# One queue for W1, another order of the first products, and another order of the last small operations in a conditional adapter kernel

## The chip, the cores and the metric

The kernel runs on one core of a Trainium2 chip. The metric is the time of one execution on the device in microseconds (us); before the change it is 321.33 us, the median of three runs (320.34 to 324.42). One further execution was recorded by the hardware profiler, and all views come from it.

## The reference

128 samples x[b] of 128 rows by 512 columns (float32), each with a language number between 0 and 9. The language picks its own weights: W1 (512 by 128), W2 (128 by 512), and the vectors b1, b2, gamma, beta. For each sample:

```
h       = relu(x @ W1[lang] + b1[lang])            # 128 x 128, the product "down"
adapted = h @ W2[lang] + b2[lang]                  # 128 x 512, the product "up"
y       = x + adapted
normed  = (y - mean(y)) / sqrt(var(y) + 1e-5)      # over the 512 columns
out     = x + normed * gamma[lang] + beta[lang]
```

## The kernel before

**What is resident.** All ten languages' W1 and W2 stay in SBUF (`w1`, `w2`, 2.62 MB each), and so do beta, gamma and b2, each spread over all 128 partitions (`beta_b`, `gamma_b`, `b2_b`). The spreading is done at the start by `spread(r, copier)` (L152): for each of the 30 rows TensorE multiplies a selection column with the rows' parts into a PSUM buffer of the pool `p_y` (five buffers), and VectorE or ScalarE copies that to SBUF (L161, L159). x comes in groups of four samples (1 MB each) into four buffers; the first group comes in two halves (`load_part`, L82).

**The start's transfers.** Two engines issue transfers, each on a queue of its own: SyncE (q1 in the profile) and ScalarE (q10). W1 goes in four parts of 655,360 bytes, one for each slice of 128 rows of all ten languages; its contiguous runs are 512 bytes long. The loop at L95 puts parts 0 and 1 on SyncE and parts 2 and 3 on ScalarE. SyncE's queue goes on with x's second half, W2 in two transfers, and x_1, x_2, x_3 (L100 to L109). x and W2 have runs of 2 KB.

**One sample's work.** `stage_w1` (L184): ScalarE copies the sample's W1 from `w1` at a place given by a register, so it needs all four parts. `transpose_x` (L189): four transposes on TensorE into the single buffer of pool `p_x`. `copy_xT` (L194): ScalarE brings them to SBUF. `down` (L211): four products into the single buffer of pool `p_h`. `relu` (L221) on ScalarE. `up` (L225): the product with W2, into a `p_y` buffer, with a small product for b2 first where `b2_by_matmul` says so (samples 0 to 3, then every fourth). `residual` (L235), `negative_mean`, `scale` and `finish` are VectorE's, `square` and `deviation` ScalarE's; GpSimd adds x and b2 beforehand (`add_b2`, L198), and x and beta (`add_beta`, L204). The reciprocal standard deviation comes out of the five small VectorE steps `rstd_1` to `rstd_5`, for two samples at once; for the last four samples `rstd_of(b, n)` (L307) does step n for one sample alone.

**What sets the order.** The tile framework places the waits. Nearly every instruction is passed through `keep` (L43), which holds it behind the one written before it on the same engine; so each engine's order is the written one.

**The start's order (L425 to L453).** Idle products (`spin`) for TensorE, the transposes of sample 0, rows 0 to 21 of the spreading with the transposes of sample 1 between them, `stage_w1` of samples 0 and 1, four more idle products, then a loop over samples 0 to 2: `down`, the transposes two samples on, `relu`, `copy_xT`, up to three rows of the spreading (copied by VectorE), `stage_w1` two samples on. After it `up(0)`, `up(1)`, `down(3)`, `relu(3)`, `stage_w1(5)`. The main loop (L455) begins with `up(2)` and the transposes of sample 4.

**The end (`tail`, L355).** The last five samples leave the loop's pattern. At its last step, the sample called b + 1 is the last (127) and b the one before; their small steps stand between the scalings (`scale`) and the two last `finish_last` (L350), each of which is followed by a store.

Of the kernel before, what the change touches and what calls it, by code (L numbers as in the profile page):

```python
# [16 lines left out]
P = 128  # L17
# [6 lines left out]
def cond_resid_kernel(ctx: ExitStack, tc: tile.TileContext, x, itok, W1, b1, W2, b2, gamma, beta, out):  # L24
# [8 lines left out]
    nc = tc.nc  # L33
    B, S, H = x.shape
# [8 lines left out]
    def keep(ins):  # L43

        engine = ins.ins.engine
        if engine in last:
            tc.add_manual_dep(ins.ins, last[engine], behind, reason="kept order")
        last[engine] = ins.ins.name
        return ins
# [27 lines left out]
    w1 = const.tile([P, L, KC, A], FP, name="w1")  # L77
# [15 lines left out]
    nc.vector.memset(warm, 1.0)  # L93
    keep(nc.scalar.activation(warm, warm, AF.Sqrt))
    for k in range(KC):  # L95
        queue = nc.sync if k < 2 else nc.scalar
        keep(
            queue.dma_start(out=w1[:, :, k, :], in_=W1[:, k * P : (k + 1) * P, :].rearrange("l p a -> p l a"))
        )
    load_part(2, G)  # L100
    for l in range(0, L, 5):
        keep(
            nc.sync.dma_start(
                out=w2[:, l * H : (l + 5) * H].rearrange("p (l h) -> p l h", l=5),
                in_=W2[l : l + 5].rearrange("l a h -> a l h"),
# [46 lines left out]
    def spread(r, copier):  # L152
        t = (beta_b, gamma_b, b2_b)[r // L]
        row = p_y.tile([P, H], FP, tag="y", name=f"row_{r}")
        pick_r = pick[:, r : r + 1].to_broadcast([96, P])
        keep(nc.tensor.matmul(row, lhsT=pick_r, rhs=parts[:96, :], start=True, stop=True))  # L156
        dst = t[:, r % L * H : (r % L + 1) * H]
        if copier is nc.scalar:
            keep(nc.scalar.copy(dst, row))  # L159
        else:  # L160
            keep(nc.vector.tensor_copy(dst, row))  # L161
# [4 lines left out]
    def lid(b, engine):  # L166
        g = b // G
        if (g, engine) not in lids:
            loads, vals = nc.values_load_multi_w_load_instructions(  # L169
                lang[0:1, g * G : (g + 1) * G],  # L170
                engines=[engine],
                min_val=0,
                max_val=L - 1,
                skip_runtime_bounds_check_because="clamped on the chip to 0..L-1 above",
            )
            for ins in loads:
                keep(ins)
            lids[g, engine] = vals
        return lids[g, engine][b % G]
# [4 lines left out]
    def stage_w1(b):  # L184
        w1s[b] = wp.tile([P, KC, A], FP, tag="w1s", name=f"w1s_{b}")
        src = w1.rearrange("p l k a -> p (l k a)")[:, bass.ds(lid(b, ET.Activation) * (KC * A), KC * A)]
        keep(nc.scalar.copy(w1s[b].rearrange("p k a -> p (k a)"), src))  # L187
# [23 lines left out]
    def down(b):  # L211
        phs[b] = p_h.tile([P, P], FP, tag="h", name=f"ph_{b}")
        for k in range(KC):
            keep(
                nc.tensor.matmul(  # L215
                    phs[b], lhsT=w1s[b][:, k, :], rhs=xT[b][:, k, :], start=(k == 0), stop=(k == KC - 1)
                )
            )
        del xT[b], w1s[b]

    def relu(b):  # L221
        hT[b] = tp.tile([P, P], FP, tag="hT", name=f"hT_{b}", bufs=6)
        keep(nc.scalar.activation(hT[b], phs.pop(b), AF.Relu, bias=b1T[:, bass.ds(lid(b, ET.Activation), 1)]))  # L223
# [11 lines left out]
    def residual(b):  # L235
        r = xb(b) if b2_by_matmul(b) else rs.pop(b)
        s = st.tile([P, 1], FP, tag="sum", name=f"sum_{b}")
        keep(nc.vector.scalar_tensor_tensor(ys[b], ys[b], 1.0, r, ALU.mult, ALU.add, accum_out=s))  # L238
        sums[b] = s

    def negative_mean(b):
        nmeans[b] = st.tile([P, 1], FP, tag="nmean", name=f"nmean_{b}")
        keep(nc.vector.tensor_scalar(nmeans[b], sums.pop(b), -1.0 / H, None, ALU.mult))  # L243
# [15 lines left out]
    def rstd_1(g):  # L259
        stats[g] = p_s.tile([P, 6], FP, tag="s", name=f"stat_{g}")  # L260
        keep(nc.vector.tensor_scalar(stats[g][:, 0:2], ssqs.pop(g), -0.5 / H, -0.5 * EPS, ALU.mult, ALU.add))

    def rstd_2(g):
        y0s[g] = st.tile([P, 2], FP, tag="y0", name=f"y0_{g}")
        keep(nc.vector.reciprocal(y0s[g], sds.pop(g)))

    def rstd_3(g):
        keep(nc.vector.tensor_tensor(stats[g][:, 2:4], stats[g][:, 0:2], y0s[g], ALU.mult))

    def rstd_4(g):  # L270
        keep(nc.vector.tensor_tensor(stats[g][:, 4:6], stats[g][:, 2:4], y0s[g], ALU.mult))  # L271

    def rstd_5(g):
        rstds[g] = st.tile([P, 2], FP, tag="rstd", name=f"rstd_{g}")
        keep(
            nc.vector.scalar_tensor_tensor(rstds[g], stats.pop(g)[:, 4:6], 1.5, y0s.pop(g), ALU.add, ALU.mult)
        )

    def scale(b):
        v = lid(b, ET.DVE)  # L280
        keep(
            nc.vector.scalar_tensor_tensor(  # L282
                ys[b], ys[b], nmeans.pop(b), gamma_b[:, bass.ds(v * H, H)], ALU.add, ALU.mult
            )
        )
# [20 lines left out]
    def rstd_of(b, n):  # L306

        if not ends:
            ends["t"] = p_s.tile([P, 32], FP, tag="s", name="stat_ends")
        t = ends["t"][:, 8 * (b % 4) : 8 * (b % 4) + 3]  # L310
        if n == 1:
            keep(nc.vector.tensor_scalar(t[:, 0:1], ssqs.pop(b), -0.5 / H, -0.5 * EPS, ALU.mult, ALU.add))
        elif n == 2:
            y0s[b] = st.tile([P, 1], FP, tag="y0", name=f"y0_{b}")
            keep(nc.vector.reciprocal(y0s[b], sds.pop(b)))
        elif n < 5:
            keep(nc.vector.tensor_tensor(t[:, n - 2 : n - 1], t[:, n - 3 : n - 2], y0s[b], ALU.mult))
        else:
            rstds[b] = st.tile([P, 1], FP, tag="rstd", name=f"rstd_{b}")
            keep(nc.vector.scalar_tensor_tensor(rstds[b], t[:, 2:3], 1.5, y0s.pop(b), ALU.add, ALU.mult))  # L320
# [26 lines left out]
    def store_last(b):  # L347
        nc.sync.dma_start(out=out[b], in_=os[b // 2][:, b % 2, :])
# [6 lines left out]
    def tail(b):  # L355
        p = E // 2
        if b == E + 3:
            rstd_of(b - 2, 4)
        residual(b)
        if b == E + 1:  # L360
            rstd_1(p)
            rstd_2(p)
            negative_mean(b)
            rstd_3(p)
            scale(E - 1)
            rstd_4(p)
            rstd_5(p)
            shift(E)
            finish(E - 2)
            store(p - 1)  # L370
            deviation_of(b)
            by_pool(E, False)
        elif b == E + 2:
            negative_mean(b)
            rstd_of(b - 1, 1)
            rstd_of(b - 1, 2)
            finish_last(E - 1)
            store_last(E)
            rstd_of(b - 1, 3)
            deviation_of(b)  # L380
        elif b == E + 3:
            rstd_of(b - 2, 5)
            negative_mean(b)
            shift(b - 2)
            residual(b + 1)
            negative_mean(b + 1)
            by_pool(b - 2, False)
            store_last(b - 2)
            rstd_of(b - 1, 1)
            rstd_of(b - 1, 2)  # L390
            rstd_of(b - 1, 3)
            scale(b - 1)
            deviation_of(b)
            rstd_of(b - 1, 4)
            rstd_of(b - 1, 5)
            scale(b)
            deviation_of(b + 1)
            by_pool(b - 1, True)
            store_last(b - 1)
            rstd_of(b, 1)  # L400
            rstd_of(b, 2)
            rstd_of(b, 3)
            scale(b + 1)
            rstd_of(b, 4)
            rstd_of(b + 1, 1)
            rstd_of(b + 1, 2)
            rstd_of(b, 5)
            rstd_of(b + 1, 3)
            rstd_of(b + 1, 4)
            finish_last(b)  # L410
            rstd_of(b + 1, 5)
            finish_last(b + 1)


    def spin(n, width):
        idle = p_s.tile([P, H], FP, tag="s", name="idle")
        for _ in range(n):
            keep(
                nc.tensor.matmul(
                    idle[:, :width], lhsT=ones, rhs=ones[:, 0:1].to_broadcast([P, width]), start=True, stop=True  # L420
                )
            )
# [12 lines left out]
            spin(1, H // 2)  # L435
    stage_w1(0)
    stage_w1(1)
    spin(4, H)
    for b in range(3):
        down(b)  # L440
        if b < 2:
            transpose_x(b + 2)
        relu(b)
        if b < 2:
            copy_xT(b + 2)
        for r in range(22 + 3 * b, min(25 + 3 * b, R)):
            spread(r, nc.vector)
        stage_w1(b + 2)
    up(0)
    up(1)  # L450
    down(3)
    relu(3)
    stage_w1(5)  # L453

    for i in range(3, B + U):  # L455
        if i < B and i % G == 0 and i // G + 3 < NG:
            load_x(i // G + 3)
        b = i - U - 1
# [20 lines left out]
        p = g - 1  # L479
# [79 lines left out]
```

## Time and profile before

| | |
|---|---|
| median of three runs | 321.33 us |
| the profiled execution | 321.27 us |
| its span, first to last instruction | 319.5 us |
| PE (TensorE) busy | 304.8 us, 95% |
| DVE (VectorE) busy | 302.8 us, 95% |
| ACT (ScalarE) busy | 283.3 us, 89% |
| POOL (GpSimd) busy | 280.7 us, 88% |
| mean DMA rate | 228 GB/s |
| mean granted TensorE clock | 0.991 |

PE stands for TensorE's products, PEld for its weight loads, DVE for VectorE, ACT for ScalarE, POOL for GpSimd, SP for SyncE. L187 is line 187 of the kernel. A line of the timeline gives the start, the duration, the engine, the line of code, the operation, what it writes and reads, and in brackets the engine's idle time before it and what ended that. Operations of one engine overlap in part, so distances are taken from start to start. In the names of tiles buffer numbers are left out: `w<-in_L_cond_W_dram` stands for W1 as well as W2, `b_b` for `b2_b`, `row` for a row of the spreading, `py` for the product up, `ph` for the product down.

### The profile page before, as it was taken

The page shows a single profiled execution, that of the slowest core. Times are in us where ns is not written, and L with a number is a line of the kernel's source. Part 1 is how long each engine was busy: PE and PEld are TensorE (multiplying, and loading weights), DVE is VectorE, ACT ScalarE, POOL GpSimd, SP SyncE. Part 2 cuts the span into 40 slices and gives each one's busy share as a digit, 9 for nine tenths or more (in the row PEclk, how much of TensorE's full clock was granted, in tenths as well). Part 3 has the DMA queues.
Part 4 walks back from the last instruction along what each step waited for, and adds up shares of the span by engine and source line. Part 5 has one row for each costly group of instructions (what it writes and reads, how often), then busy time and mean ns, then how long its engine had stood idle before and what let it go on. Part 6 is the DMA issues. An engine that isn't in the chain of part 4 may idle for free.

```text
span 319.5 us, 7184 instructions
## 1 busy us (share of the span) xinstructions
PE 304.8 (95%) x1890; PEld 226.4 (71%) x1890; DVE 302.8 (95%) x1003; ACT 283.3 (89%) x718; POOL 280.7 (88%) x234
## 2 busy tenths in 40 slices
PE   8979999999999999999999999999999999999960
PEld 3566777777777777777777777777777777777740
DVE  5956999999999999999999999999999999999995
ACT  2556989999999999999999999999999999999972
POOL 1306999999999999999999999999999999999874
PEclk9999999999999999999999999999999999999996
DMA  7997566777566766777666666777666666733234
GB/s 209 321 385 276 199 253 210 265 264 254 205 213 220 241 240 220 257 262 261 224 211 214 233 242 221 248 263 260 223 214 214 223 249 223 244 132 134 111 114 173
DMA packets 40987, 72.89 MB, mean 228 GB/s; under 512 B 1737, under 2 KB 6868, under 8 KB 40946
## 3 DMA queue, kind: packets, MB, share of 16 engines
q1 hardware_dynamic: 38294, 71.07, 64.8%
q10 hardware_dynamic: 2652, 1.36, 1.7%
q8 instruction: 16, 0.26, 0.3%
q14 instruction: 25, 0.20, 0.2%
HBM read 38.86 MB, written 33.55 MB: 227 GB/s over the span
## 4 chain that ended last, share of the span: by engine, by line
POOL 46%; issue 26%; POOLq 9%; DVE 7%; PE 5%; DMA 5%; ACT 1%; ACTq 0%; DVEq 0%
POOL o L209 31%; POOL r L202 14%; POOLq L169 8%; DMA w<-in_L_cond_W_dram 5%; DVE py L282 2%; PE ph L215 2%; DVE py L238 1%; DVE o L291 1%; PE py L232 1%; PE pxT L192 1%; POOLq L209 1%; DVE o L352 1%; PE row L156 1%; ACT w1s L187 0%; PE py L231 0%
## 5 line engine op out<-in xcount | busy, mean ns | idle before, releaser
L209 POOL TENSOR_TENSOR o<-x,beta_b 128x512 f32<-128x512 f32 x128 | 161.8, 1277 | 10.6 <-DVE beta_b L161 10.6
L215 PE MATMUL ph<-xT,w1s 128*128 128x128 f32 x1024 | 135.5, 275 | 1.9 <-ACT w1s L187 1.8
L202 POOL TENSOR_TENSOR r<-x,b_b 128x512 f32<-128x512 f32 x93 | 118.7, 1276 | 21.0 <-DMA x<-in_x_dram 12.1
L232 PE MATMUL py<-w,hT 128*128 x256 | 131.0, 593 | 0.2 <-DVE o L291 0.2
L215 PEld LDWEIGHTS ph<-xT,w1s 128*128 128x128 f32 x1024 | 124.7, 192 | 4.0 <-ACT w1s L187 2.3
L192 PEld LDWEIGHTS pxT<-ident,x 128*128 128x128 f32 x512 | 64.0, 141 | 66.6 <-issue 44.4
L282 DVE SCALAR_TENSOR_TENSOR py<-py,nmean,gamma_b 128x512 f32<-128x512 f32 x126 | 94.7, 751 | 0.0
L291 DVE SCALAR_TENSOR_TENSOR o<-py,rstd,o 128x512 f32<-128x512 f32 x122 | 90.4, 741 | 1.0
L250 ACT ACTIVATE sq<-py,nmean 128x512 f32<-128x512 f32 x124 | 85.2, 687 | 3.0 <-DVE nmean L243 1.8
L196 ACT COPY xT<-pxT 128x512 f32<-128x512 f32 x128 | 73.7, 576 | 11.9 <-PE pxT L192 9.7
L187 ACT COPY w1s<-w 128x512 f32 x128 | 79.4, 621 | 2.1 <-DMA w<-in_L_cond_W_dram 2.0
L192 PE MATMUL pxT<-ident,x 128*128 128x128 f32 x512 | 77.0, 273 | 0.7 <-ACT xT L196 0.7
L238 DVE SCALAR_TENSOR_TENSOR py<-py,r 128x512 f32<-128x512 f32 x93 | 64.7, 696 | 2.4 <-PE pxT L192 0.7
L223 ACT ACTIVATE hT<-ph,b1T 128x128 f32<-128x128 f32 x128 | 47.4, 371 | 4.1 <-PE ph L215 4.1
L232 PEld LDWEIGHTS py<-w,hT 128*128 128x128 f32 x256 | 41.7, 192 | 2.7 <-issue 0.6
L238 DVE SCALAR_TENSOR_TENSOR py<-py,x 128x512 f32<-128x512 f32 x35 | 24.2, 692 | 2.4 <-PE py L232 1.8
L250 ACT ACTIVATION_READ_ACCUMULATOR sq<-py,nmean 128x1 f32 x124 | 25.3, 204 | 0.0
L256 ACT ACTIVATE sd<-ssq,eps 128x2 f32<-128x2 f32 x62 | 18.3, 296 | 2.1
L243 DVE TENSOR_SCALAR nmean<-sum 128x1 f32<-128x1 f32 x128 | 18.8, 147 | 0.2
L231 PE MATMUL py<-parts,pick 96*128 96x512 bf16 x35 | 13.3, 381 | 0.0
L238 DVE DVE_READ_ACCUMULATOR py<-py,r 128x1 f32 x93 | 13.1, 141 | 0.0
L271 DVE TENSOR_TENSOR stat<-stat,y 128x2 f32<-128x2 f32 x62 | 12.8, 206 | 0.0
(54 smaller groups left out, 118.1 us busy)
## 6 DMA issues: line engine op xcount, KB each, us to landing
x<-in_x_dram SPq DMA_DIRECT2D x31, 1024.0 KB, 6.0
out_dram<-o SPq DMA_DIRECT2D x61, 512.0 KB, 3.3
w<-in_L_cond_W_dram SPq DMA_DIRECT2D x2, 1280.0 KB, 15.6
out_dram<-o SPq DMA_DIRECT2D x6, 256.0 KB, 2.0
w<-in_L_cond_W_dram SPq DMA_DIRECT2D x2, 640.0 KB, 6.6
w<-in_L_cond_W_dram ACTq DMA_DIRECT2D x2, 640.0 KB, 8.6
x<-in_x_dram SPq DMA_DIRECT2D x2, 512.0 KB, 3.6
rows<-in_L_cond_beta_dram ACTq DMA_DIRECT2D x1, 20.0 KB
```

Of the source, the lines that this page charges most:

```text
L187: keep(nc.scalar.copy(w1s[b].rearrange("p k a -> p (k a)"), src))
L192: keep(nc.tensor.transpose(pxs[b][:, k, :], xb(b)[:, k * P : (k + 1) * P], ident))
L196: keep(nc.scalar.copy(xT[b], pxs.pop(b)))
L202: keep(nc.gpsimd.tensor_tensor(rs[b], xb(b), b2_b[:, bass.ds(v * H, H)], ALU.add))
L209: keep(nc.gpsimd.tensor_tensor(os[g][:, j, :], xb(b), beta_b[:, bass.ds(v * H, H)], ALU.add))
L215: nc.tensor.matmul(phs[b], lhsT=w1s[b][:, k, :], rhs=xT[b][:, k, :], start=(k == 0), stop=(k == KC - 1))
L223: keep(nc.scalar.activation(hT[b], phs.pop(b), AF.Relu, bias=b1T[:, bass.ds(lid(b, ET.Activation), 1)]))
L232: keep(nc.tensor.matmul(ys[b], lhsT=hT[b], rhs=w2[:, bass.ds(v * H, H)], start=not m, stop=True))
L238: keep(nc.vector.scalar_tensor_tensor(ys[b], ys[b], 1.0, r, ALU.mult, ALU.add, accum_out=s))
L250: keep(nc.scalar.activation(sq, ys[b], AF.Square, bias=nmeans[b], accum_out=ssqs[g][:, j : j + 1]))
L282: nc.vector.scalar_tensor_tensor(ys[b], ys[b], nmeans.pop(b), gamma_b[:, bass.ds(v * H, H)], ALU.add, ALU.mult)
L291: nc.vector.scalar_tensor_tensor(o, ys.pop(b), rstds[g][:, j : j + 1], o, ALU.mult, ALU.add)
```

## The change

Three edits. All four parts of W1 are issued by SyncE, behind x's first half and ahead of its second. In the start's order there is one idle product less (three in place of four); the loop takes in sample 3, so that four products down stand ahead of the first product up; and the copies of rows 23, 26 and 29 go from VectorE to ScalarE. At the end, the small steps of the last two samples are interleaved, and all of them stand ahead of the two last `finish_last`.

```diff
--- before.py
+++ after.py
@@ -93,9 +93,8 @@
     nc.vector.memset(warm, 1.0)
     keep(nc.scalar.activation(warm, warm, AF.Sqrt))
     for k in range(KC):
-        queue = nc.sync if k < 2 else nc.scalar
         keep(
-            queue.dma_start(out=w1[:, :, k, :], in_=W1[:, k * P : (k + 1) * P, :].rearrange("l p a -> p l a"))
+            nc.sync.dma_start(out=w1[:, :, k, :], in_=W1[:, k * P : (k + 1) * P, :].rearrange("l p a -> p l a"))
         )
     load_part(2, G)
     for l in range(0, L, 5):
@@ -399,16 +398,16 @@
             store_last(b - 1)
             rstd_of(b, 1)
             rstd_of(b, 2)
+            rstd_of(b + 1, 1)
+            rstd_of(b + 1, 2)
             rstd_of(b, 3)
+            rstd_of(b + 1, 3)
             scale(b + 1)
             rstd_of(b, 4)
-            rstd_of(b + 1, 1)
-            rstd_of(b + 1, 2)
+            rstd_of(b + 1, 4)
             rstd_of(b, 5)
-            rstd_of(b + 1, 3)
-            rstd_of(b + 1, 4)
+            rstd_of(b + 1, 5)
             finish_last(b)
-            rstd_of(b + 1, 5)
             finish_last(b + 1)
 
 
@@ -435,8 +434,8 @@
             spin(1, H // 2)
     stage_w1(0)
     stage_w1(1)
-    spin(4, H)
-    for b in range(3):
+    spin(3, H)
+    for b in range(4):
         down(b)
         if b < 2:
             transpose_x(b + 2)
@@ -444,13 +443,10 @@
         if b < 2:
             copy_xT(b + 2)
         for r in range(22 + 3 * b, min(25 + 3 * b, R)):
-            spread(r, nc.vector)
+            spread(r, nc.scalar if r % 3 == 2 else nc.vector)
         stage_w1(b + 2)
     up(0)
     up(1)
-    down(3)
-    relu(3)
-    stage_w1(5)
 
     for i in range(3, B + U):
         if i < B and i % G == 0 and i // G + 3 < NG:
```

## The prediction

> **What bounds the kernel now.** I read four views: busy time by stretches, then the waits, then the timeline of ACT and PE around the longest waits, then the end on DVE. First the stretches (start:end, length, then busy time and instructions of PE, PEld, DVE, ACT, POOL, then PE's clock, the DMA share, GB/s):
>
> ```profile
> 5.00:5.50 0.50, 0.50 (x3) 0.22 (x2) 0.47 (x2) 0.00 (x0) 0.00 (x0) 1.00 1.14 346
> 6.00:12.00 6.00, 6.00 (x35) 3.53 (x34) 4.84 (x11) 3.41 (x6) 0.00 (x0) 1.00 1.19 292
> 17.00:29.00 12.00, 10.12 (x62) 7.39 (x62) 7.72 (x17) 7.23 (x16) 2.44 (x2) 1.00 1.05 386
> 36.00:300.00 264.00, 263.94 (x1676) 200.64 (x1675) 260.68 (x880) 251.24 (x647) 255.41 (x207) 1.00 0.67 228
> ```
>
> From 36 to 300 us PE has no gap: starts on the timeline give four transposes 0.44, a product down 0.89, a product up 0.86, a b2 product 0.21, so four batches cost 4 x 2.19 + 0.21 = 8.97 us, which is the period seen. DVE is nearly full, POOL does its seven operations per four batches in about 8.65 us and waits for DVE. So **the loop is bound by PE**, and a PE that enters it earlier ends earlier by as much, if what feeds it keeps up. What counts is the start and the end. The waits (engine and line, what for, us in total, times, longest):
>
> ```profile
> POOL r L202 <- DMA x<-in_x_dram: 12.1, 1, 12.1
> ACT w1s L187 <- DMA w<-in_L_cond_W_dram: 2.0, 1, 2.0
> PE ph L215 <- ACT w1s L187: 1.8, 1, 1.8
> ```
>
> The timeline of ACT, then of PE (start, us, operation, idle before it):
>
> ```profile
> 14.91 0.58 ACT L159 COPY b_b<-row 128x512 f32<-128x512 f32 x1 [0.79 <-PE row L156]
> 17.53 1.14 ACT L187 COPY w1s<-w 128x512 f32 x2 [2.04 <-DMA w<-in_L_cond_W_dram]
> ...
> 15.04 1.36 PE L419 MATMUL idle<-ones 128*128 128x256 bf16 x5
> 18.20 1.16 PE L215 MATMUL ph<-xT,w1s 128*128 128x128 f32 x8 [1.80 <-ACT w1s L187]
> ...
> 27.71 0.60 PE L192 MATMUL pxT<-ident,x 128*128 128x128 f32 x4
> ```
>
> W1 lands at 17.47. ACT is through with its copies at 15.49 and waits; PE is through with its idle products at about 16.0 and waits until 18.20. From 18.20 to 28.15 PE runs without a gap. The transpose of batch 4 (27.71) needs x_1, which landed at 26.5 (POOL's wait above ends at 26.56). Which queue moved what, from 5 to 5.5 us, then from 6 to 12 us (packets, MB, share of the engines):
>
> ```profile
> q1 hardware_dynamic: 338, 0.17, 114.1%
> ...
> q10 hardware_dynamic: 1863, 0.95, 64.7%
> q1 hardware_dynamic: 1586, 0.80, 54.6%
> ```
>
> q1 is SP's queue, q10 ACT's. At 5 to 5.5 us SP's queue was alone, with W1's packets of 512 bytes (0.17 MB / 338), at **346 GB/s**; with both queues full of them the rate was 292. From 12 us on q1 carries 2 KB packets of x and W2, and the last 0.33 MB of W1 on q10 take until 17.
>
> **What the Trainium skill says.** *DMA: Bandwidth & Descriptors*, "Queues, rings and completion order": an engine goes round robin between the queues, packet by packet. The trace agrees (8 to 10 us: 585 and 559 packets); so W1's small packets get a small share beside W2's large ones. Same page, "Issuing engines are not separate DMA queues": a second issuing engine saves only issue time. The trace goes further: the second queue cost 346 - 292 = 54 GB/s. *TensorE: Matmul & The Clock Gate*, "What's actually happening": about 3.4 us of idleness halve PE's clock. The idle 1.80 us left it at 1.00, so one idle product less is harmless. *VectorE: DVE Perf Modes*, "The DRAIN you can't avoid": the next operation waits until the pipeline is empty. The trace differs: independent small operations start 0.06 to 0.07 us apart, dependent ones about 0.19; I use those.
>
> **W1 on SP's queue.** ACT loses two issues (0.41 and 0.88 us, at 2.17 to 3.50); it then waits for PE until 7.10, so that is worth nothing. SP gains two, ahead of x's second half, W2, x_1, x_2, x_3. SP's issue waits[...] (2.52 us for x's second half), but the queue then holds data. Data: by 4.5 us 0.59 MB have moved. W1 is 2.62 MB: 0.15 by 5.0 at 305 GB/s, the rest at 346 takes 7.1, so it is through at **12.1**. Landings trail the mean of the bytes: summed microsecond by microsecond, x_1's bytes (7.41 MB in all) are through at 24.2, and it lands at 26.5, 2.3 later. W1 then lands by 14.4 at the latest, before ACT asks. x's second half (0.52 MB at 387) follows by 13.5, lands by 15.8; needed at 17.1. W2 (2.62 MB) is through at 20.2, lands by 22.5; needed at 22.95 (below). x_1 (1.05 MB) is through at **22.9**, lands at **25.2**, 1.3 earlier. Bounds of the one-queue rate: 346 seen for half a microsecond; 292 if it doesn't last (W1 13.5, x_1 26.6); 145 if a queue got no more than its half of 292.
>
> **The first product down.** ACT's register load ran at 14.9, during the last copy (0.3 to 0.53 us), so the stationary copy starts at 15.47 instead of 17.53. PE follows 0.67 us after, as now (17.53, 18.20): 16.14. The idle products, one fewer (0.21 us), are through at 15.79; four would be through at 16.0, so that edit is worth nothing. Gain **2.06 us** (1.5 if the load is not covered).
>
> **Four products down first, three copies of rows to ACT.** PE's work up to the transpose of batch 4 is the same, 9.5 us. New: between product down 2 and 3 only two row products (0.43) lie, where the single PSUM buffer of the product has to be freed by the relu: 0.2 us latency, 0.37, 0.06, which is 0.63, and ACT is late by 0.14 with its added copies (per batch relu 0.31 + xT 0.53 + row 0.53 + w1s 0.57 against PE's 1.98). Cost **0.3 us**, between 0.2 and 0.8. The copies' 3 x 0.53 us on ACT lie inside PE's stretch (ACT was busy 5.8 of the 10 us). DVE loses 3 x 0.61, but its first residual waits for the first product up: worth nothing. First product up with W2: 16.14 + 6.8 = 22.95. Transpose of batch 4: 16.14 + 9.8 = **25.95**, against 27.71, and x_1 is there at 25.2. Gain at the loop's entry **1.75 us**. The 0.84 us stall after it (one transpose buffer) stays. POOL starts 1.3 earlier; its r_4 was ready at 27.8 and used at 33.94, some 6 us of slack, so it does not take over.
>
> **The end.** DVE's last operations now:
>
> ```profile
> 312.90 0.15 DVE L312 TENSOR_SCALAR stat_ends<-ssq 128x1 f32<-128x1 f32 x1
> ...
> 313.27 0.76 DVE L282 SCALAR_TENSOR_TENSOR py<-py,nmean,gamma_b 128x512 f32<-128x512 f32 x1
> 313.94 0.15 DVE L317 TENSOR_TENSOR stat_ends<-stat_ends,y 128x1 f32<-128x1 f32 x1
> 314.13 0.16 DVE L312 TENSOR_SCALAR stat_ends<-ssq 128x1 f32<-128x1 f32 x1
> 314.20 0.15 DVE L315 RECIPROCAL y<-sd 128x1 f32<-128x1 f32 x1
> 314.33 0.16 DVE L320 SCALAR_TENSOR_TENSOR rstd<-stat_ends,y 128x1 f32<-128x1 f32 x1
> ...
> 314.80 0.75 DVE L352 SCALAR_TENSOR_TENSOR o<-py,rstd,o 128x512 f32<-128x512 f32 x1
> 315.46 0.15 DVE L320 SCALAR_TENSOR_TENSOR rstd<-stat_ends,y 128x1 f32<-128x1 f32 x1
> 315.72 0.75 DVE L352 SCALAR_TENSOR_TENSOR o<-py,rstd,o 128x512 f32<-128x512 f32 x1
> ```
>
> New order, same clock: the first two steps of both batches at 312.90, 312.96, 313.03, 313.10 (the last batch's deviation is ready at 312.95 on ACT); step 3 at 313.17 and 313.29; the scaling at 313.36; step 4 at 314.03 and 314.10; step 5 at 314.22 and 314.29; the first finish 0.26 after its rstd (as 315.46, 315.72), at 314.48, the second 0.67 later at 315.15. It was 315.72: gain **0.57 us**, between 0.3 and 0.7. The last store then leaves earlier by as much; its 3 us stay.
>
> **Sum.** 1.75 + 0.57 = 2.3 us. The profiled execution took 321.27 (span 319.5 and 1.77 around it), 0.06 below the median of 321.33, so both give **319.0 us**.
>
> **The rivals.** (1) x_1 comes no earlier: one queue keeps only 292 GB/s. Then the transpose runs at 26.65: gain 1.06 + 0.57, **319.6**. For it: 346 was seen only briefly; against: no q10 packets in that time. (2) The start's gain is lost in the loop, because DVE (260.68 of 264) or POOL takes over; the end alone stays: **320.7**. For it: DVE's busy share; against: POOL waits for DVE, DVE waited for PE early on. (3) Slower: W1's 5120 small packets in one queue, with x's second half, W2 and x_1 all behind them, run at some 218 GB/s (halfway between 145 and 292). W1 is through at 16.5, x_1 at 27.3, lands at 29.6: the transpose is 1.94 later, less 0.57: **322.6**. It decides from 247 GB/s down (x_1 at 28.2, which eats the end's gain). Against it stands the 346.
>
> **How the numbers follow.** The forecast has 0.62, rival 1 0.15, rival 2 0.13, rival 3 0.10. The forecast's own range is 318.1 to 320.0 (the stall up to 0.8, the load uncovered, the end 0.3 to 0.7). To hold 8 in 10, with the scatter of the runs before (320.34 to 324.42), it reaches from 317.9 to 321.2, over rivals 1 and 2; rival 3 is left out. A difference under 2% (6.4 us) can't be told from no change in this kernel, and no case but rival 3 at its extreme (145 GB/s, about 329) goes beyond: faster 0.02, within 0.95, slower 0.03.
>
> **What would show it.** W1's wait on ACT gone, first product down near 16.1; the DMA rate about 346 from 5 to 12 us on q1 alone; POOL's wait for x_1 ending near 25.2; a wait of 0.2 to 0.3 us of the fourth product down on the relu; the transposes of batch 4 near 26; PE without gaps after that; the two last finishes 0.67 apart. A rate under 292 on one queue, or a PE wait for W2 or x_1, makes it wrong.

## The result

Timed beside each other on one chip, 22 executions each: before 322.74 us (320.34 to 324.91), after 320.95 us (320.03 to 322.48). The ratio is 0.9954 (95% interval 0.9933 to 0.9975), so the change saves some 1.5 us, between 0.8 and 2.2, where 2.3 were forecast (the two medians alone lie 1.8 apart). That is less than the 2% below which the prediction saw no way to tell a change from none; with this many executions it can be told. The profiled execution of after has a span of 318.8 us, 0.7 less than the profiled one of before, and one term of the sum came out with the wrong sign.

**The start.** Busy time by stretches of after (columns as in the prediction):

```profile
5.00:5.50 0.50, 0.50 (x3) 0.23 (x2) 0.47 (x2) 0.00 (x0) 0.00 (x0) 1.00 1.15 350
6.00:12.00 6.00, 6.00 (x35) 3.54 (x34) 4.82 (x11) 3.42 (x6) 0.00 (x1) 1.00 1.20 290
17.00:29.00 12.00, 11.08 (x68) 7.68 (x68) 6.67 (x17) 8.50 (x20) 2.39 (x2) 1.00 1.05 386
36.00:300.00 264.00, 263.94 (x1673) 200.30 (x1673) 260.62 (x884) 252.07 (x647) 256.10 (x208) 1.00 0.66 226
```

From 36 to 300 us nothing changed: PE is full, as before. The new thing is the second line. From 6 to 12 us one queue alone (q1 moved all of the 1.74 MB in that time) ran at 290 GB/s, the same as the two queues of before together (292), although 350 still stand in the line above it. What that did is seen on POOL's timeline, then on PE's:

```profile
26.61 1.26 POOL L201 TENSOR_TENSOR r<-x,b_b 128x512 f32<-128x512 f32 x1 [12.13 <-DMA x<-in_x_dram]
```

```profile
16.39 1.16 PE L214 MATMUL ph<-xT,w1s 128*128 128x128 f32 x8 [0.23 <-ACT w1s L186]
...
21.35 0.60 PE L155 MATMUL row<-parts,pick 96*128 96x512 bf16 x2
21.97 1.16 PE L214 MATMUL ph<-xT,w1s 128*128 128x128 f32 x8
...
26.59 0.63 PE L191 MATMUL pxT<-ident,x 128*128 128x128 f32 x4 [0.22 <-DMA x<-in_x_dram]
27.89 0.66 PE L191 MATMUL pxT<-ident,x 128*128 128x128 f32 x4 [0.68 <-ACT xT L195]
```

The first product down comes 1.8 us earlier (16.39, before 18.20), ACT's wait for W1 is gone, and the fourth product down starts 0.62 after the two rows ahead of it, about 0.2 later than those rows need. But x_1 lands when it did before: POOL's wait for it ends at 26.61 (before 26.56). The transposes of batch 4 (the prediction calls a sample a batch) run into it and start at 26.59; with them the main loop is entered. Of the 1.8 us, 1.12 reach the loop (27.71 - 26.59). At PE's last products up 1.00 is left (307.23 before, 306.23 after).

**The end.** DVE's timeline of after from the first small step on:

```profile
311.90 0.15 DVE L311 TENSOR_SCALAR stat_ends<-ssq 128x1 f32<-128x1 f32 x1
311.96 0.15 DVE L314 RECIPROCAL y<-sd 128x1 f32<-128x1 f32 x1
312.16 0.16 DVE L311 TENSOR_SCALAR stat_ends<-ssq 128x1 f32<-128x1 f32 x1
312.23 0.15 DVE L314 RECIPROCAL y<-sd 128x1 f32<-128x1 f32 x1
312.35 0.37 DVE L316 TENSOR_TENSOR stat_ends<-stat_ends,y 128x1 f32<-128x1 f32 x2
313.03 0.76 DVE L281 SCALAR_TENSOR_TENSOR py<-py,nmean,gamma_b 128x512 f32<-128x512 f32 x1 [0.31 <-issue]
313.70 0.35 DVE L316 TENSOR_TENSOR stat_ends<-stat_ends,y 128x1 f32<-128x1 f32 x2
314.09 0.22 DVE L319 SCALAR_TENSOR_TENSOR rstd<-stat_ends,y 128x1 f32<-128x1 f32 x2
314.35 1.41 DVE L351 SCALAR_TENSOR_TENSOR o<-py,rstd,o 128x512 f32<-128x512 f32 x2
```

The last line holds both finishes; the second starts some 0.66 after the first, near 315.01. From the first small step to that is 3.11 us; before it was 2.82 (312.90 to 315.72). The new order costs 0.29 us instead of gaining 0.57. The last sample's first step comes 0.20 after the operation before it, not 0.07, and the scaling comes 1.13 after the first step, not 0.46. So the two traces account for 1.0 - 0.3 = 0.7 us, the difference of the spans. The remaining 0.8 of the measured 1.5 us is not in these two executions; the last group of experiments looks for it.

### The profile page after: what moved, and what is told of

Same layout as the page of the kernel before. It is cut to its first block, busy times and chain, and to the rows that moved or that the text cites. A ratio compares the mean times of both kernels' runs of the same rounds, so it can differ in the third digit from the quotient of the medians.

```text
span 318.8 us, 7184 instructions
## 1 busy us (share of the span) xinstructions
PE 305.1 (96%) x1889; PEld 226.0 (71%) x1889; DVE 300.7 (94%) x1000; ACT 285.5 (90%) x721; POOL 280.6 (88%) x234
## 5 line engine op out<-in xcount | busy, mean ns | idle before, releaser
L201 POOL TENSOR_TENSOR r<-x,b_b 128x512 f32<-128x512 f32 x93 | 118.8, 1277 | 20.0 <-DMA x<-in_x_dram 12.1
L195 ACT COPY xT<-pxT 128x512 f32<-128x512 f32 x128 | 73.8, 577 | 12.1 <-PE pxT L191 10.1
L249 ACT ACTIVATION_READ_ACCUMULATOR sq<-py,nmean 128x1 f32 x124 | 25.2, 203 | 0.0
```

What stands on the lines that cost most here:

```text
L195: keep(nc.scalar.copy(xT[b], pxs.pop(b)))
L201: keep(nc.gpsimd.tensor_tensor(rs[b], xb(b), b2_b[:, bass.ds(v * H, H)], ALU.add))
L249: keep(nc.scalar.activation(sq, ys[b], AF.Square, bias=nmeans[b], accum_out=ssqs[g][:, j : j + 1]))
```

## The experiments

All times are medians beside runs of before on the same chip (322.6 to 322.9 us, spans of 318.6 to 323.2, median 320.8 to 321.1). "Span" is the median span. Lines L… in the fences are those of the kernel at hand, a few off those of before.

| kernel | us, range, executions | ratio to before, 95% | span |
|---|---|---|---|
| queue_only | 320.15 (319.58 to 320.56, 8) | 0.992 (0.9895 to 0.9945) | 318.4 |
| order_only | 323.48 (320.90 to 324.97, 20) | 1.0017 (0.9993 to 1.004) | 321.7 |
| tail_only | 323.02 (320.97 to 325.26, 12) | 1.0011 (0.9981 to 1.0041) | 321.3 |
| old_tail | 320.18 (319.60 to 320.58, 8) | 0.9919 (0.9896 to 0.9941) | 318.3 |
| after_again | 320.88 (320.36 to 322.01, 20) | 0.9954 (0.9933 to 0.9974) | 318.9 |
| tail_own | 320.68 (320.22 to 321.43, 20) | 0.9958 (0.9941 to 0.9976) | 318.7 |
| spin12 | 322.22 (321.22 to 323.56, 20) | 0.9996 (0.9973 to 1.0019) | 319.7 |
| w1_lang | 320.77 (320.11 to 322.22, 20) | 0.9948 (0.9928 to 0.9967) | 318.9 |
| x1_halves | 319.37 (318.96 to 319.92, 6) | 0.9908 (0.9877 to 0.994) | 317.5 |
| w1_2kb | 323.22 (322.65 to 324.08, 20) | 1.0004 (0.9985 to 1.0022) | 321.4 |
| w1_2kb_halves | 322.93 (322.23 to 323.96, 20) | 1.0014 (0.9996 to 1.0032) | 320.8 |
| old_tail_b | 320.09 (319.69 to 320.55, 15) | 0.9916 (0.9889 to 0.9944) | 318.2 |
| x1_halves_b | 319.27 (319.10 to 319.44, 6) | 0.9893 (0.9844 to 0.9942) | 317.5 |
| queue_halves | 319.44 (319.32 to 319.73, 10) | 0.9905 (0.987 to 0.9941) | 317.7 |

The first four ran on one chip, the next four on a second, x1_halves, w1_2kb and w1_2kb_halves on a third, the last three on a fourth.

### One edit at a time

**queue_only**: before, with W1 on one queue and nothing else.

```diff
-        queue = nc.sync if k < 2 else nc.scalar
         keep(
-            queue.dma_start(out=w1[:, :, k, :], ...)
+            nc.sync.dma_start(out=w1[:, :, k, :], ...)
```

> The kernel before with all four parts of W1 on SyncE's queue and nothing else. Theory (x_1's landing sets when the loop begins): first product down near 16.4, DMA rate 290 GB/s from 6 us until W1 is through, x_1 landing at 26.5, the transposes of batch 4 at 26.6, span 1.0 to 1.1 us shorter than before. Rival (the new order of the products is what gains): the transposes of batch 4 stay near 27.7 and the span is unchanged within 0.2.

It has the whole gain, 0.8%, with a first product down at 16.55. Its median span is 2.7 us below before's, where 1.0 to 1.1 were expected; the two profiled ones are 1.4 apart (why the medians differ by more comes last). Its timeline of PE shows where the old order meets the next arrival:

```profile
22.50 1.10 PE L231 MATMUL py<-w,hT 128*128 x2 [0.18 <-DMA w<-in_L_cond_W_dram]
...
26.48 0.60 PE L191 MATMUL pxT<-ident,x 128*128 128x128 f32 x4
```

The first product up now waits for W2, and the transposes of batch 4 come at 26.48. Its DMA rate from 6 to 12 us is 292 GB/s.

**order_only**: the start's order of after, with W1 on two queues and the tail of before.

```diff
-    spin(4, H)
-    for b in range(3):
+    spin(3, H)
+    for b in range(4):
...
-            spread(r, nc.vector)
+            spread(r, nc.scalar if r % 3 == 2 else nc.vector)
...
-    down(3)
-    relu(3)
-    stage_w1(5)
```

> The kernel before with the start's order changed alone (four products down first, three copies on ScalarE, one idle product less), W1 on two queues, the old tail. Theory: W1 lands at 17.5 as before, the fourth product down waits 0.2 us for the relu, the transposes of batch 4 come 0.2 us later than in the kernel before (27.9), span 0.1 to 0.3 us longer. Rival (the new order gains because the VectorE copies are off the path): span 0.3 to 0.6 us shorter.

No gain. Its profile shows something that neither of the first two had. PE's timeline, then the stretch from 20 to 25 us:

```profile
19.09 1.42 PE L215 MATMUL ph<-xT,w1s 128*128 128x128 f32 x8 [3.14 <-ACT w1s L187]
```

```profile
20.00:25.00 5.00, 5.00 (x27) 4.02 (x26) 1.81 (x3) 3.01 (x7) 0.00 (x0) 0.67 1.05 387
```

W1 landed at about 18.4 here, 0.9 later than in the profile of before. PE had idled 3.14 us, and its clock, which the line of before had at 1.00, then fell to 0.67 on average over five microseconds (in stretches of one microsecond it is 0.50 from 20 to 23). The Trainium skill's *TensorE: Matmul & The Clock Gate*, "What's actually happening", puts the clock at half after an idle window of about 3.4 us, and says that the window runs freely; a pause of one length could then be harmless once and not another time. The two traces fit that, though 3.14 us is a little less than the page's window: 1.80 us of idling left the clock at 1.00, 3.14 us halved it. So this execution says little about the order itself; in the timed runs order_only is level with before.

**tail_only**: before, with only the new order of the last small operations (the second hunk of the diff).

```diff
             rstd_of(b, 2)
+            rstd_of(b + 1, 1)
+            rstd_of(b + 1, 2)
             rstd_of(b, 3)
+            rstd_of(b + 1, 3)
             scale(b + 1)
...
```

> The kernel before with the new order of the last small operations alone. Theory (the new tail costs time): the last scaling starts 0.7 to 0.8 us after the last pair's first step instead of 0.37, the second finish 3.1 us after it instead of 2.82, so the span is 0.3 us longer than before. Rival (the tail gains the 0.57 us of the prediction, and the loop loses it): the span is 0.5 us shorter. A third reading, that the gap of 0.3 us ahead of the last scaling is an accident of where the instructions lie: the gap is gone here and the span is equal to that of before within 0.1.

```profile
312.71 0.15 DVE L312 TENSOR_SCALAR stat_ends<-ssq 128x1 f32<-128x1 f32 x1
...
312.97 0.16 DVE L312 TENSOR_SCALAR stat_ends<-ssq 128x1 f32<-128x1 f32 x1
...
313.57 0.76 DVE L282 SCALAR_TENSOR_TENSOR py<-py,nmean,gamma_b 128x512 f32<-128x512 f32 x1
...
314.89 1.41 DVE L352 SCALAR_TENSOR_TENSOR o<-py,rstd,o 128x512 f32<-128x512 f32 x2
```

On this timeline of DVE the second finish starts near 315.55, 2.84 after the first step: worth nothing (before 2.82), which is the third of the readings. The scaling comes 0.86 after the first step, and the 0.31 us of "issue" ahead of it in after is not there.

**old_tail**: after, with the tail of before (the same hunk undone).

```diff
-            rstd_of(b + 1, 1)
-            rstd_of(b + 1, 2)
             rstd_of(b, 3)
-            rstd_of(b + 1, 3)
             scale(b + 1)
...
```

> The changed kernel with the old order of the last small operations. Theory: the span is 0.3 us shorter than that of the changed kernel (318.5 against 318.8), 1.0 shorter than before. Rival (the new tail gains 0.57): the span is 0.5 longer than that of the changed kernel (319.4).

Level with queue_only (320.18 and 320.15), and its tail takes 2.83 again. So the edit of the queue makes the gain, and the order adds nothing to it. The new tail takes 0.3 back in the trace of after, nothing in that of tail_only.

### The tail: a shared tile

The small steps of both samples write columns of one tile, `stat_ends`. **after_again** is the unchanged kernel after, **tail_own** gives the last sample's steps a tile of their own, in SBUF.

```diff
         t = ends["t"][:, 8 * (b % 4) : 8 * (b % 4) + 3]
+        if b == B - 1:
+            if n == 1:
+                ends["own"] = st.tile([P, 3], FP, tag="own", name="stat_own", bufs=1)
+            t = ends["own"]
```

> The changed kernel once more, beside the three others of this call. Theory (the new tail costs 0.0 to 0.3 us): its median lies 0.0 to 0.4 us above that of the changed kernel with the old tail (320.18 us in the earlier call), all runs within 1.5 us of each other. Rival (the new tail costs about 1 us, as the two ratios of the separate calls, 0.9954 and 0.9919, would have it): 1 us above it, 321.2.

> The changed kernel, the last sample's small steps in a tile of their own in SBUF instead of columns of the tile that all four last samples share. Theory (the two samples' steps wait for each other because they share that tile): the last sample's step 1 follows 0.07 us behind the step before it instead of 0.20, the last scaling starts 0.5 to 0.6 us after the pair's first step instead of 0.86 to 1.13, the second finish 2.5 us after it instead of 2.84 to 3.11, span 0.3 us shorter than that of the changed kernel. Rival (VectorE's sequencer limits the rate of small operations, whatever tile they use): the scaling stays 0.8 us or more behind, no gain.

after_again repeats after: ratio 0.9954, the same tail of 3.11 with the same 0.31 gap. Its median lies 0.70 above that of old_tail, more than the theory's 0.4 and less than the rival's 1.0. The tail explains 0.28 of that (3.11 against 2.83). The rest stays open: the two never ran on one chip, and w1_lang (below), which has the old tail and ran beside after_again, has the same median span of 318.9.

DVE's timeline of tail_own:

```profile
312.00 0.15 DVE L315 TENSOR_SCALAR stat_ends<-ssq 128x1 f32<-128x1 f32 x1
312.06 0.15 DVE L318 RECIPROCAL y<-sd 128x1 f32<-128x1 f32 x1
312.13 0.13 DVE L315 TENSOR_SCALAR stat_own<-ssq 128x1 f32<-128x1 f32 x1
...
312.37 0.39 DVE L320 TENSOR_TENSOR stat_own<-stat_own,y 128x1 f32<-128x1 f32 x1
312.68 0.75 DVE L281 SCALAR_TENSOR_TENSOR py<-py,nmean,gamma_b 128x512 f32<-128x512 f32 x1
...
313.41 0.57 DVE L320 TENSOR_TENSOR stat_own<-stat_own,y 128x1 f32<-128x1 f32 x1
313.90 0.15 DVE L323 SCALAR_TENSOR_TENSOR rstd<-stat_ends,y 128x1 f32<-128x1 f32 x1
...
314.15 1.41 DVE L355 SCALAR_TENSOR_TENSOR o<-py,rstd,o 128x512 f32<-128x512 f32 x2
```

The last sample's first step now follows 0.07 behind its predecessor, as the prediction had it, so the 0.20 came from the shared tile. The new tile also lies in SBUF and not in PSUM, but that alone doesn't make the difference: in before, a sample's first step into `stat_ends` in PSUM starts at 310.87, 0.07 behind an operation (310.80) that writes another tile. The scaling comes 0.68 after the first step, and the tail takes 2.81 (2.5 had been expected). That beats after's tail by 0.30 in the trace and 0.2 us in the medians, but only draws level with the old order: steps 3 and 4 on the SBUF tile last 0.39 and 0.57 us and hold back the next operation by 0.31 and 0.49, where the same steps on the old tile last about 0.16. The new order never won in any form tried.

### The rate: queues, addresses or packets

**w1_lang**: old_tail with W1 in ten transfers, one for each language, still in 512-byte runs. It changes the addresses that are read at one time, not the packets.

```diff
-    for k in range(KC):
-        keep(nc.sync.dma_start(out=w1[:, :, k, :], in_=W1[:, k * P : (k + 1) * P, :]...))
+    for l in range(L):
+        keep(nc.sync.dma_start(out=w1[:, l], in_=W1[l].rearrange("(k p) a -> p k a", k=KC)))
```

> The changed kernel with the old tail and W1 in ten transfers, one for each language (all 512 rows of one language, 512-byte runs as before), on SyncE's queue. Theory (the fall from 346 to 290 GB/s belongs to 512-byte packets once some 60 of them per engine are through, whatever the addresses): 346 GB/s until about 6 us, then 290, W1 through near 13.4, span as with four transfers (318.4). Rival (it is the addresses: ten blocks 256 KB apart in turn): 330 to 346 GB/s until W1 is through near 12.2, x_1 landing 1 us earlier.

297 GB/s from 6 to 12 us, and x_1 lands near 26.36 (26.59 in after), not 1 us earlier, so the addresses are not it. The median span of 318.9 is 0.5 longer than expected. In the trace the loop, from its entry to the last products up, takes 0.35 longer than in old_tail (279.97 against 279.62); more on that below. **w1_2kb**: old_tail with rows 4p to 4p+3 of W1 in partition p, so that runs are 2 KB long (two transfers); to match, the transposes read every fourth column of x. The result is the same computation.

```diff
-    for k in range(KC):
-        keep(nc.sync.dma_start(out=w1[:, :, k, :], in_=W1[:, k * P : (k + 1) * P, :]...))
+    for l in range(0, L, 5):
+        keep(nc.sync.dma_start(out=w1[:, l : l + 5].rearrange("p l k a -> p l (k a)"),
+                               in_=W1[l : l + 5].rearrange("l (p k) a -> p l (k a)", k=KC)))
...
-            keep(nc.tensor.transpose(pxs[b][:, k, :], xb(b)[:, k * P : (k + 1) * P], ident))
+            keep(nc.tensor.transpose(pxs[b][:, k, :], xb(b).rearrange("s (p k) -> s k p", k=KC)[:, k, :], ident))
```

> The changed kernel with the old tail, W1 with each partition's four rows taken next to each other (rows 4p to 4p+3 instead of p, p+128, ...), so that its runs are 2 KB long, in two transfers; the transposes of x read every fourth column to match. Theory (the 512-byte packets at 290 GB/s are what the prediction sized wrongly): 387 GB/s from 4.5 us, W1 through near 11.3 us, W2 and x_1 2.1 us earlier than with the old tail alone, x_1 landing at 24.2 to 24.5, the transposes of batch 4 at 26.0 to 26.5 with no wait, span 0.2 to 0.6 us shorter. Rival (reading every fourth column slows TensorE's transposes): their start-to-start of 0.44 us for four grows, and the span grows by 128 times the difference, above 325 us at 0.05 us each.

The stretch from 6 to 12 us, POOL's first addition of x_1, and the group of weight loads of the transposes (busy us in total, mean ns of one, idle time before), of w1_2kb; the last line is that group in old_tail:

```profile
6.00:12.00 6.00, 6.00 (x36) 3.67 (x35) 5.04 (x11) 3.43 (x7) 0.18 (x1) 1.00 1.03 375
```

```profile
24.97 1.27 POOL L204 TENSOR_TENSOR r<-x,b_b 128x512 f32<-128x512 f32 x1 [10.66 <-DVE py L240]
```

```profile
L194 PEld LDWEIGHTS pxT<-ident,x 128*128 128x128 f32 x512 | 80.5, 202 | 59.7 <-issue 36.8 <-ACT w1s L189 21.6 <-ACT xT L198 1.3
```

```profile
L191 PEld LDWEIGHTS pxT<-ident,x 128*128 128x128 f32 x512 | 64.1, 141 | 66.7 <-issue 44.4 <-ACT w1s L186 18.3 <-ACT xT L195 4.0
```

375 GB/s, and x_1 is there by 24.97, 1.6 earlier than in after: the rate goes with the length of the packets. The kernel is slower for another reason. The strided transposes' weight loads take 202 ns on average instead of 141, and four transposes take 0.47 us from start to start instead of 0.44. Over 128 samples that is 3.8 us; the span is 3.0 longer than old_tail's although the transposes of batch 4 came 0.4 earlier (26.06). This edit is no way to a faster kernel.

### Who holds the entry of the loop

**x1_halves**: old_tail with x_1 in two transfers of two samples, so that samples 4 and 5 can start on the first.

```diff
-        keep(nc.sync.dma_start(out=t, in_=x[g * G : (g + 1) * G]...))
+        for lo in (0, 2) if g == 1 else (0,):
+            hi = lo + 2 if g == 1 else G
+            keep(nc.sync.dma_start(out=t[:, lo:hi, :], in_=x[g * G + lo : g * G + hi]...))
```

> The changed kernel with the old tail, x_1 loaded in two halves of two samples. Theory (the landing of x_1 holds the transposes of batch 4 and, with them, the loop): the first half lands 1.0 to 1.4 us earlier, near 25.1, TensorE has no wait for x, the transposes of batch 4 start 0.0 to 0.4 us earlier than with x_1 whole (26.0 to 26.5), GpSimd's first sum with b2 starts near 25.2, span 318.2, 0.2 to 0.4 shorter than with the old tail alone. Rival (x_1 is not what holds the loop): no difference within 0.1 us.

Two executions in which the first product down came equally early tell what x_1 costs. PE's timeline of w1_lang (x_1 whole), then of x1_halves:

```profile
15.71 1.16 PE L212 MATMUL ph<-xT,w1s 128*128 128x128 f32 x8 [0.36 <-ACT w1s L184]
...
26.36 0.63 PE L189 MATMUL pxT<-ident,x 128*128 128x128 f32 x4 [0.52 <-DMA x<-in_x_dram]
```

```profile
15.63 1.16 PE L216 MATMUL ph<-xT,w1s 128*128 128x128 f32 x8 [0.22 <-ACT w1s L188]
...
25.44 0.60 PE L193 MATMUL pxT<-ident,x 128*128 128x128 f32 x4
```

With x_1 whole PE waits for it; in halves it doesn't, and the entry is 0.92 earlier. (Expected were 0.0 to 0.4; the median span came out 0.8 below old_tail's on another chip, where 0.2 to 0.4 were expected.) The same two samples' halves in w1_2kb, where x_1 was in time already, are **w1_2kb_halves** (both diffs together).

> Both of these edits together. Theory: with W1's long runs x_1 is in time whole, so halving it adds nothing: within 0.2 us of the kernel with long runs alone. Rival (the landing still decides): 0.3 us or more shorter than it.

At the entry nothing more is gained: POOL starts on x_1 at 22.59, the transposes come at 26.14 (26.06 without halves), PE's last products up at 308.83 (308.76). The medians still differ by 0.29 us, more than the 0.2 expected and just short of the rival's 0.3, and the median spans by 0.6. The two traces do not show why.

But why does the first product down come at 15.6 once and at 16.7 another time, in kernels that do the same up to then? PE's timeline of after, then of x1_halves, at the very start:

```profile
2.43 4.05 PE L418 MATMUL idle<-ones 128*128 128x512 bf16 x9
6.27 0.77 PE L191 MATMUL pxT<-ident,x 128*128 128x128 f32 x4
```

```profile
2.43 3.00 PE L420 MATMUL idle<-ones 128*128 128x512 bf16 x9
5.27 0.60 PE L193 MATMUL pxT<-ident,x 128*128 128x128 f32 x4
```

The same nine idle products take 4.05 us or 3.00, and in these two executions the first product down moves with them. One by one the products start 0.43 us apart at first and 0.22 apart later. *TensorE: Matmul & The Clock Gate* in the Trainium skill, "What you observe", has the clock rise about 4 us into the activity, half a microsecond earlier or later from run to run. Here the first product starts at 1.18, and the change comes at 4.4 in x1_halves and after 6.27 in after, which is 3.2 us and more than 5 us in, a wider spread than the page's. (That it is the clock is the page's account; the view's column for PE's clock reads 1.00 throughout.) It is not the only thing that moves the start: in after_again the change comes at 4.4 too, but the transposes wait 0.46 for x and the rows of the spreading 0.99 for VectorE, which had waited 1.7 for beta, gamma and b2, so that the first product down comes at 16.93, the latest of all with one queue. So x1_halves against old_tail could have been luck of the start, and both were run again side by side, with a third kernel, **queue_halves**: queue_only with x_1 in halves, so the same without the new order of the products.

> The kernel after with the tail of before, once more, as the yardstick for the next two on the same chip. Both theories: the transposes of batch 4 run at the later of two times, 9.8 us after the first product down (which came between 15.6 and 16.7 in the profiles so far, as TensorE's start came early or late) and x_1's landing at about 26.4. Ratio to before about 0.992 to 0.994.

> The same with x_1 in two halves, once more, timed beside it. Theory: x_1's landing sets the entry of the loop whenever the first product down comes early, so the halves save up to 1.0 us there and nothing where it comes late: its median is 0.3 to 0.9 us below old_tail_b, its fastest executions about 0.6 to 1.0 below. Rival: the 1.2 us between the first two profiles came from TensorE's earlier start (first product down 15.63 against 16.67), and the two kernels time the same within 0.2 us.

> W1 on one queue and x_1 in halves, but the start's order and the tail of before (three products down ahead of the first up). Theory: the order of after covers W2, whose landing at 22.5 the old order meets: with the first product down at 15.6 to 16.6 the product up is due at 21.4 to 22.4 and waits 0.1 to 1.1 us for W2, so that the transposes of batch 4 run at about 26.4 and the kernel is 0.1 to 0.8 us slower than x1_halves_b. Rival: the order costs more (0.2 to 0.3 us on the relu) than it covers, and this kernel is level with x1_halves_b or up to 0.3 us faster.

The halves win 0.82 us, and the ranges do not meet (319.10 to 319.44 against 319.69 to 320.55), so it was not the start alone. The two profiled executions do not show it at the entry: the transposes are at 26.06 with halves and at 26.07 without, since the start was late in the first (first product down 16.25) and early in the second (15.83). The difference of their spans, 0.4, arises in the loop.

queue_halves shows what the new order is for. Its PE timeline:

```profile
22.42 1.10 PE L233 MATMUL py<-w,hT 128*128 x2 [1.05 <-DMA w<-in_L_cond_W_dram]
...
26.41 0.60 PE L193 MATMUL pxT<-ident,x 128*128 128x128 f32 x4
```

The old order waits 1.05 us for W2, as expected for an early start, and enters the loop at 26.41. Yet it is only 0.17 us slower than x1_halves_b, and the ranges overlap. The theory is right on the wait and at its lower end on the price; a part is made up in the loop, where its last products up come 279.02 us after the entry, against 279.21 in x1_halves_b and 279.3 to 280.0 in the other kernels with one queue (w1_2kb and w1_2kb_halves aside, whose transposes are slower).

The traces show where that arises. From the transposes of sample 28 (near 80 us) to those of sample 124 each profiled execution (the same two aside) takes 215.5 to 215.6 us, only old_tail_b 215.7. From the entry to sample 28 they take 53.24 to 54.20 us. In all four with 53.24 or 53.25 (queue_halves, order_only, tail_only, spin12) POOL had started on x_1 at least 1.3 us ahead of the entry; in the ten others it started at most 1.15 ahead, and they take 53.43 or more. In six of these ten DVE waits 0.3 to 0.7 us for POOL between 36 and 60 us, as in after:

```profile
42.77 0.70 DVE L237 SCALAR_TENSOR_TENSOR py<-py,r 128x512 f32<-128x512 f32 x1 [0.63 <-POOL r L201]
```

So a late x_1 seems to cost twice, at PE's transposes and through POOL's late start. No run here changes POOL's start alone, so the second part is not shown: queue_halves has such a wait too (0.43) and loses nothing.

### The 0.8 us that the two traces lack

**spin12**: before, with twelve idle products in place of four while W1 is awaited.

```diff
-    spin(4, H)
+    spin(12, H)
```

> The kernel before with twelve idle products instead of four ahead of the first product down (8 more of 0.213 us, ending near 17.8), nothing else. Theory (in the kernel before TensorE sits idle for 1.8 to 3.2 us until W1 lands, and after the long waits its clock falls, which is what spreads its runs over 321.3 to 324.4 us): granted clock 0.991 in nearly every run, median 321.3 to 321.8 us against 322.9, no run above 322.5. Rival (the spread has another cause): clock and spread as in the kernel before, median 322.9 or more.

In before, the spans of 70 executions on that chip go from 318.7 to 323.2, with PE's mean clock at about 0.99 in the 27 shortest (up to 319.8) and from 0.977 to 0.987 in the others. With the idle products the clock stays at 0.987 to 0.992 in all 20, and the spans end at 320.9. So the low clock comes from PE's idling ahead of W1, and with it go the spans above 320.9. The median was missed, though (322.22, 0.4 below before). The median span fell by more, from 320.8 to 319.7, but what the timed runs have on top of the span grew from 1.8 to 2.5 us at the median, and no run here tells why. The spans also still spread over 2.1 us, where the kernels with W1 on one queue spread over about 1. That W1 on two queues lands at changing times fits (17.5 in before and in spin12, 17.8 in tail_only, 18.4 in order_only), but it is argued, not shown.

On the same chip after_again ran at spans of 318.6 to 319.5. Its shortest is hardly shorter than before's (318.6 and 318.7), its median 1.9 lower. So a good part of what the change brought is most likely that W1 is always there in time.

## Why the prediction was right and wrong

- **What bounds the kernel: right.** PE is full from 36 to 300 us in both, and 1.12 us at the entry became 1.00 at the last products up. The rest went where the prediction's second rival had looked, but small: DVE waited once, 0.6 us, for POOL at 42.77. "Some 6 us of slack, so it does not take over" was therefore too safe, and "ends earlier by as much" holds only to about 0.5 us: the loop's first 54 us differ by up to 1.0 between executions.
- **"The rest at 346": wrong, and the largest miss.** This is the term that failed. 346 held to about 6 us in both kernels, then packets of 512 bytes went at 290 to 297, on one queue or two (before 292, queue_only 292, after 290, w1_lang 297), and 2 KB packets in the same place at 375 (w1_2kb). W1 was through near 13.5, not at 12.1. So the second queue had cost nothing of the rate, and the reading "the trace goes further: the second queue cost 54 GB/s" took for an effect of the queue what came at the same moment as the second queue. The bound of 292 that the prediction kept gave x_1 at 26.6; it landed at 26.6. By the prediction's own last sentence, a rate under 292 and PE's wait for x_1 were the signs of its being wrong; both came.
- **First product down: nearly right.** 16.39 for 16.14, because the stationary copy waited for the last spread row as well (15.72 for 15.47).
- **Order of the products, 0.3 us: right in size.** The stall at the fourth product down is 0.2. Whether it brings anything was not asked: it covers a wait for W2 of up to 1.05, worth at most some 0.2 us once x_1 is in halves (the ranges overlap), nothing with x_1 whole.
- **Transposes of batch 4 at 25.95, x_1 there at 25.2: wrong, by the rate.** 26.59 with a wait for x. This is the first rival (26.65), which had a chance of 0.15. Entry gain 1.12 instead of 1.75.
- **The end, 0.57 us, "between 0.3 and 0.7": wrong, sign included.** It was 0.0 in tail_only and -0.3 in after. The sum took the steps of the two samples for independent; they share a tile, and the last sample's first step comes 0.20 behind instead of 0.07 (tail_own shows it), the scaling comes 0.86 to 1.13 behind instead of 0.46. A loss was not in that range, though a line of before that the prediction showed gave the warning: the last sample's first step (314.13) stood 0.19 behind the other sample's fourth (313.94), which it needs nothing from. The 0.31 us of "issue" in after, absent in tail_only, stays open.
- **"One idle product less is harmless", "the idle 1.80 us left it at 1.00": true of that execution only.** The sum was made against one profiled execution, 319.5 us, among the shorter of a kernel that runs up to 323.2. The term that it lacks is W1 arriving late and PE's clock falling. It is most likely what brings the measured 1.5 us above the 0.7 of the two traces: spin12 shows that the low clock comes from the idling, not how much of the 0.8 it is.
- **Which rival came true:** the first, with the tail lost as well. By its own sum with a tail of -0.3 the gain would be 1.06 - 0.3 = 0.8, which is the difference of the spans to 0.1. That the measured 1.5 us stands nearer to the forecast than this is luck: the missing term happens to make up for part of the two misses.

The best kernel tried is x1_halves: 319.27 us and 319.37 on two chips, 0.9893 (0.9844 to 0.9942) and 0.9908 (0.9877 to 0.994) of before.

## What to carry to other kernels

When a wait is taken from the front, look up which arrival the next consumer waits for, and move that too: here the first product down came 1.8 us earlier and only 1.1 of it was used until x_1 was split, so that its first half came in time. A rate that stands for half a microsecond is no rate for seven; use the one that the trace holds for as long as the transfer will take. Before summing small operations as independent, see whether they write the same tile, and read the spread of the timed runs as well as one profile, for a stall that differs from one execution to the next isn't in it.

## What was not expected of the hardware

- 512-byte packets from HBM to SBUF began at 346 to 350 GB/s (27 ns each in the trace) and went over to 290 to 292 (33 ns) at about 6 us, in before and after alike; 2 KB packets ran at 375 to 387. Why just then, no run here tells.
- Transposing float32 with every fourth column as the weights costs 202 ns for a weight load instead of 141.
- TensorE's rate at the start doubles at a moment that differs by some 2 us from one execution to the next (4.4 us, or later than 6.27): the same nine idle products took 3.00 or 4.05 us.
